# A routed mixture of experts on one core: six single tiles in place of seven, the index table built earlier and in another layout

## The chip, the core and the metric

The kernel runs on one core of a Trainium2 chip. Its engines are TensorE (PE; its weight loads are shown apart as PEld), VectorE (DVE), ScalarE (ACT), GpSimd (POOL) and SyncE (SP). The metric is device time in microseconds (us). A profiled execution gives a trace with the start, the length and the wait of each instruction.

## The reference

`x` has 64 x 64 = 4096 tokens of H = 256 values, and there are E = 8 experts with hidden width M = 512. Each token goes through its two likeliest experts; all is f32.

```python
var = jnp.mean(x * x, axis=-1, keepdims=True)
xn = rms_w * (x * jax.lax.rsqrt(var + EPS))
gate = xn @ wg_W + wg_b + (genre_embed @ gg_W + gg_b)
topk_w, topk_i = jax.lax.top_k(jax.nn.softmax(gate, axis=-1), 2)
cw = jnp.sum(jax.nn.one_hot(topk_i, E) * topk_w[..., None], axis=-2)
h1 = jax.nn.relu(jnp.einsum('bsh,ehm->bsem', x, W1) + b1)
h2 = jax.nn.relu(jnp.einsum('bsem,emn->bsen', h1, W2) + b2)
out_e = jnp.einsum('bsen,enh->bseh', h2, W3) + b3
return x + jnp.einsum('bseh,bse->bsh', out_e, cw)
```

## The kernel before

**Tiles and units.** The 8192 pairs of a token and an expert are sorted by expert and cut into tiles of 128. Token `p * 32 + i` lies in partition `p`, column `i`. The *first part* is columns 0 to 7 (1024 tokens), the rest is columns 8 to 31. The first part is routed first, from its own gates, so that work can begin early: the first `F` units are *single tiles*, unit `u` holding the first 128 pairs of expert `u` from the first part (`firsts` has 128 for experts below `F`, 0 for the others). All other pairs form the *wide units*, after the gates of the rest are known: each expert's remaining tiles are cut into units of four tiles (512 tokens), pairs of tiles, and one last unit of 1 to 4 tiles whose width is a multiple of 32 tokens. `SHAPES` lists the sets of widths for which an arm of the program is written out; which arm runs is read at run time (`nex`). `NREST` is the largest number of tiles that the wide units can have.

**Layers.** A single runs three plain layers (`layer1`: 8 products 128x128, `layer2`: 16 of them, `layer3`: 4 products 128x256). A wide unit runs layers 1 and 2 (`Fast`) with seven products of blocks in place of eight, over half the unit's tokens each (Winograd's form of Strassen's scheme; `fold` makes the sums of weight blocks, `mix` those of data blocks, `p(k)` is a product, `c11`, `c12`, `c22` add them). Layer 3 of a unit of four tiles is of that kind too (`Wide`), of smaller units it is plain. Layer 3 of a unit is done amid the next unit's work.

**The way to the first wide unit.** A generator, `rest()`, issues VectorE's work on the rest in pieces, and `until(label)` in a unit's step runs it up to a label: choice of experts, counts, kinds of units, places. Then the table "slot to token" is built: for each chunk of 16 token columns VectorE makes a one-hot of a pair's row within its tile (`ohl`, from `iotx`), a one-hot of its tile (`ohh`, from `whole`, which `spread_map` makes), and `ohv = ohh * tokw`, with the token numbers `tokw`. TensorE sums 64 products of `ohl` and `ohv` (`table(n)`, the first n columns) in PSUM bank 7. VectorE turns the sum into `idxR`, and GpSimd gathers rows of `x` by it, one indirect DMA per tile: `xgE` for wide unit `F`, the end of `big` for unit `F + 1`, and so on in turn. The rows of unit `F` are transposed on TensorE (eight transposes, four tiles by two halves of H). Those of later units go through DRAM (`stow`, `shuffle`) and VectorE's stream transpose. The weights of the rest's pairs (`pB.weights`, `pB.spread`) are written to `cwdR` in DRAM and gathered by tile (`gather_cw`).

**Order.** Everything is written out by hand (`tc.manual_schedule()`): each engine runs its instructions in the order of the code. `head_step(u)` is the step of singles 0 to `F - 2`, `step(F - 1)` that of the last single, `step_fast(u)` that of a wide unit. SP's queue carries the loads of weights, the copies of `x` into the output (`fill`), the streamed W1 and W3 of the first wide units, and `stow` and `shuffle`; GpSimd's carries gathers and the scatters that add results into the output (`send`). `give` scales a tile's result on VectorE and sends it; `held` keeps some of them for later. A scatter waits for that of the unit before.

Of the kernel before, what the change touches and what calls it, by code (L numbers as in the profile page):

```python
# [52 lines left out]
def kernel(  # L53
# [37 lines left out]
    F = E - 1  # L91
# [556 lines left out]
    def rest():  # L648
# [134 lines left out]
        for c in range(NCH):  # L783
            b0 = HW + (c % 3) * (LW + HW) + LW
            ohv = bigf[:, b0 : b0 + HW].bitcast(F16).rearrange("p (g t) -> p g t", g=GC)
            if c:
# [1 line left out]
            V.tensor_tensor(ohh, whole, hi16[:, cols(c)].unsqueeze(2).to_broadcast([P, GC, NREST]), ALU.is_equal)
# [1 line left out]
            V.tensor_tensor(ohv, ohh, tokw[:, i0 : i0 + GC], ALU.mult)  # L790
# [3 lines left out]
        V.tensor_scalar(sa, tab, 0.0, -1.0, ALU.is_gt, ALU.mult)  # L794
# [15 lines left out]

    def spread_map():
# [981 lines left out]
```

## Time and profile before

| what | value |
|---|---|
| median of 3 runs | 448.67 us (448.43 to 448.75) |
| the profiled execution | 448.61 us |
| its span, first to last instruction | 446.9 us |
| granted TensorE clock | 0.999 |
| busy: PE, PEld, DVE, ACT, POOL | 98%, 91%, 83%, 54%, 63% |
| indirect gathers of x for wide units | 60 |
| indirect gathers of x for singles | 7 |

Rows of a timeline read: start in us, duration in us, engine, line, operation, output <- inputs, shape, number of records merged, and in brackets the idle time before with what ended it. An f32 product is two records. Records overlap on TensorE, so a row's duration is longer than the distance to the next row's start.

### The profile page before, as it was taken

How to read it: one execution, taken by the hardware profiler on the slowest of the kernel's cores; microseconds unless marked ns; L12 is line 12 of the kernel's file. 1: busy time of each engine (PE TensorE's matmuls, PEld its weight loads, DVE VectorE, ACT ScalarE, POOL GpSimd, SP SyncE). 2: the span in 40 equal slices, each digit the busy share in tenths (PEclk: the TensorE clock that was granted, in tenths of full speed). 3: DMA queues.
4: the chain of work that ended last, by engine and by line, in shares of the span. 5: the costliest groups of instructions: out<-in, count | busy, mean ns of one | idle time of the engine just before them, and what ended most of it. 6: DMA issues, size and time to landing. Idle time of an engine off the chain costs nothing. (4 is left out here: it accounts for less than half of the span.)

```text
span 446.9 us, 9223 instructions
## 1 busy us (share of the span) xinstructions
PE 438.7 (98%) x2941; PEld 408.6 (91%) x2941; DVE 369.5 (83%) x967; ACT 242.2 (54%) x572; POOL 279.8 (63%) x237
## 2 busy tenths in 40 slices
PE   9999998999999999999999999999999999999995
PEld 8699997889898999989899999999999889999994
DVE  6898957697979888897979797988877879889962
ACT  5855533547382746555564737474454465655561
POOL 7846316778788877575858483848857447764323
PEclk9999999999999999999999999999999999999999
DMA  8999999579568575455547363736756545766312
GB/s 310 331 352 393 369 364 354 142 229 216 175 126 200 118 162 150 120 120 150 120 126 150 85 150 70 172 92 145 164 149 137 143 117 130 186 169 168 72 15 50
DMA packets 75983, 78.11 MB, mean 175 GB/s; under 512 B 35471, under 2 KB 64114, under 8 KB 75796
## 3 DMA queue, kind: packets, MB, share of 16 engines
q1 hardware_dynamic: 49376, 42.51, 30.0%
q0 software_dynamic: 14912, 17.60, 22.8%
q10 hardware_dynamic: 11636, 17.32, 11.9%
q8 instruction: 25, 0.41, 0.4%
q14 instruction: 34, 0.28, 0.2%
HBM read 61.81 MB, written 20.25 MB: 184 GB/s over the span
## 5 line engine op out<-in xcount | busy, mean ns | idle before, releaser
L1349 POOL DMA_INDIRECT out_dram<-ys,idxR x60 | 97.9, 1632 | 88.6 <-DVE ys L1335 46.8
L1166 PE MATMUL pb<-hid,big 128*128 128x256 f32 (+7 forms) x456 | 84.6, 329 | 0.0
L1187 ACT ACTIVATE hid<-hid,bb 128x256 f32<-128x256 f32 (+12 forms) x152 | 73.1, 530 | 15.5 <-DVE hid L1184 6.3
L874 POOL DMA_INDIRECT cg<-cwdR,idxR x60 | 67.4, 1123 | 19.9 <-issue 17.7
L1166 PEld LDWEIGHTS pb<-hid,big 128*128 128x128 f32 x456 | 72.1, 191 | 4.9 <-issue 0.8
L1175 ACT COPY q1s<-pb 128x512 f32<-128x512 f32 (+7 forms) x57 | 27.5, 482 | 62.1 <-PE pb L1166 61.2
L1166 PE MATMUL pb<-mixB,big 128*128 128x256 f32 (+7 forms) x304 | 56.3, 328 | 0.0
L1175 ACT COPY big<-pb 128x512 f32<-128x512 f32 (+7 forms) x57 | 27.5, 482 | 52.1 <-PE pb L1166 52.1
L1166 PE MATMUL pb<-hotA,big 128*128 128x256 f32 (+7 forms) x304 | 53.2, 328 | 0.0
L1288 PE MATMUL pb<-w3r,hid 128*128 128x256 f32 (+1 forms) x216 | 51.2, 381 | 0.0
L1166 PEld LDWEIGHTS pb<-mixB,big 128*128 128x128 f32 x304 | 48.5, 191 | 2.8
L1166 PEld LDWEIGHTS pb<-hotA,big 128*128 128x128 f32 x304 | 47.9, 191 | 2.9
L1166 PE MATMUL pb<-mixX,iotx 128*128 128x256 f32 (+7 forms) x228 | 46.9, 328 | 0.0
L874 POOL DMA_INDIRECT xgE<-in_x_dram,idxR x32 | 35.8, 1119 | 17.6 <-DVE ib L802 8.2
L1288 PEld LDWEIGHTS pb<-w3r,hid 128*128 128x128 f32 (+1 forms) x216 | 39.1, 190 | 5.2 <-issue 0.8
L1166 PEld LDWEIGHTS pb<-mixX,iotx 128*128 128x128 f32 x228 | 37.4, 191 | 2.5 <-ACT q1s L1175 0.2
L874 POOL DMA_INDIRECT big<-in_x_dram,idxR x28 | 32.2, 1149 | 8.5 <-issue 7.9
L1187 ACT ACTIVATE hid<-pb,bb 128x256 f32<-128x256 f32 (+7 forms) x76 | 27.8, 417 | 15.3 <-PE pb L1166 12.6
L1166 PE MATMUL pb<-xT,w1r 128*128 128x256 f32 (+7 forms) x152 | 31.2, 328 | 0.0
L929 DVE STREAM_TRANSPOSE xT<-gTs 128x256 f32<-128x256 f32 x56 | 29.5, 632 | 0.0
L1067 PE MATMUL pb<-hid,w2a 128*128 128x128 f32 x224 | 27.1, 276 | 0.0
L1067 PEld LDWEIGHTS pb<-hid,w2a 128*128 128x128 f32 x224 | 26.4, 192 | 0.3
(342 smaller groups left out, 841.8 us busy)
## 6 DMA issues: line engine op xcount, KB each, us to landing
w3r<-in_L_cond_W_dram ACTq DMA_DIRECT2D x17, 512.0 KB, 4.7
w2a<-in_L_cond_W_dram SPq DMA_DIRECT2D x8, 1024.0 KB, 13.7
w1r<-in_L_cond_W_dram ACTq DMA_DIRECT2D x16, 512.0 KB
w1r<-in_L_cond_W_dram SPq DMA_DIRECT2D x10, 512.0 KB, 9.5
w3r<-in_L_cond_W_dram SPq DMA_DIRECT2D x9, 512.0 KB, 12.3
big<-in_x_dram SPq DMA_DIRECT2D x8, 512.0 KB, 5.4
gTs<-scr SPq DMA_DIRECT2D x8, 512.0 KB, 4.5
out_dram<-in_x_dram SPq DMA_DIRECT2D x4, 768.0 KB
```

What stands on the lines that cost most here:

```text
L874: return nc.gpsimd.indirect_dma_start(out=dst, out_offset=None, in_=src, in_offset=bass.IndirectOffsetOnAxis(ap=index(b), axis=0), bounds_ ...
L929: V.transpose(xT[:, :, s0 + k, :].rearrange("p c (b k) -> p k c b", b=SQ), shs[:, s0 + k].rearrange("p k (a c) -> p k c a", a=SQ),)
L1067: nc.tensor.matmul(ph, lhsT=w2[:, m, ts(n, P)], rhs=hid[0][:, m, 0:BT], start=(m == 0), stop=(m == MC - 1))
L1166: nc.tensor.matmul(bank[:, ts(n, self.w)], lhsT=w[:, c, ts(n, P)], rhs=x[:, c], start=new and n == 0 and c == 0, stop=n == HB - 1 and c == ...
L1175: nc.scalar.copy(self.q[(1, 6, 5).index(k)], self.tall(self.X if k == 5 else self.U))
L1187: nc.scalar.activation(out, src, AF.Relu, bias=ww[self.u][1][:, self.l, n : n + 1])
L1288: nc.tensor.matmul(sums(u, k)[0 : cols.stop - cols.start], lhsT=hid[1][:, n, cols], rhs=w3[:, n, :], start=(i == 0), stop=(i == MC - 1))
L1349: add = nc.gpsimd.indirect_dma_start(out=orows, out_offset=bass.IndirectOffsetOnAxis(ap=index(b)[0:n], axis=0), in_=y[0:n], in_offset=None ...
```

## The change

`F` goes from 7 to 6. Expert 6 loses its single tile, and its pairs all go to wide units; `SHAPES` is drawn up anew for this (26 rows as before; one shown). In `whole`, `tokw`, `ohh` and `ohv` the axes are exchanged: 16 token columns are now innermost and tiles outside, so a product's moving operand `ohv[:, :, g]` is read with a step of 16 elements of two bytes. Table products and their one-hot rows are placed earlier against the units: chunk 0 ahead of layer 2 of unit 4, chunks 1 and 2 inside it, chunk 3 after layer 1 of unit 5. The weights of the rest and their spread come before the indices, on VectorE with the DMA on SP's queue, not on GpSimd after the gathers. The copy of the first part's weights into `cw8B` moves to the head of the program. In the first wide unit the transposes are done two tiles at a time, with half a layer 3 and products 1 and 2 between.

```diff
-    (5, 6, (16, 15, 15, 14, 12, 11, 10, 9)),
+    (5, 6, (16, 16, 15, 15, 14, 11, 10, 9)),
...
-    F = E - 1
+    F = E - 2
...
-    whole = const.tile([P, GC, NREST], F16, name="whole")
+    whole = const.tile([P, NREST, GC], F16, name="whole")
...
-                [[1, NI], [0, NREST]],
+                [[0, NREST], [1, NI]],
...
-        def spread(self, cwd, cw8, i0):
+        def spread(self, cwd, cw8, i0, eng=nc.gpsimd, queue=nc.gpsimd):
...
-            V.tensor_tensor(ohh, whole, hi16[:, cols(c)].unsqueeze(2).to_broadcast([P, GC, NREST]), ALU.is_equal)
+            V.tensor_tensor(ohh, whole, hi16[:, cols(c)].unsqueeze(1).to_broadcast([P, NREST, GC]), ALU.is_equal)
             i0 = c * GC % NI
-            V.tensor_tensor(ohv, ohh, tokw[:, i0 : i0 + GC], ALU.mult)
+            V.tensor_tensor(ohv, ohh, tokw[:, :, i0 : i0 + GC], ALU.mult)
             for g in range(GC):
-                mms.append((ohls[c][:, :, g], ohv[:, g, :], c * GC + g))
+                mms.append((ohls[c][:, :, g], ohv[:, :, g], c * GC + g))
             yield f"chunk{c}"
+        pB.weights()
+        pB.spread(cwdR, cw8B, 0, V, nc.sync)
+        yield "spread"
...
-        pB.weights()
-        nc.gpsimd.tensor_copy(cw8B[:, 0:NA, :], pA.cw8)
-        pB.spread(cwdR, cw8B, 0)
-        yield "spread"
...
+    def transpose_two(u, k0):
+        tps = [PB[4], PB[7]]
+        for k in (k0, k0 + 1):
+            for c in range(HC):
+                g = xgR[(u - F) % 2][:, k]
                 nc.tensor.transpose(tps[c][:, ts(k, BT)], g.rearrange("p (r c) -> p c r", c=HC)[:, c], ident)
+        for c in range(HC):
+            (nc.scalar.copy if c else V.tensor_copy)(
+                xT[:, c, k0 : k0 + 2, :], tps[c][:, k0 * BT : (k0 + 2) * BT].rearrange("p (s t) -> p s t", s=2)
+            )
...
+    KNOWN = 5
...
-            layer3_of(u - 1, range(HB))
             ranks_of_rest()
-            layer3_of(u - 1, range(HB, MC))
             until("kinds")
...
+        elif u == 4:
+            until("chunk0")
+            table(GC)
+            until("chunk1")
+            until("chunk2")
+            layer2(u, {2: lambda: table(2 * GC), 3: lambda: table(3 * GC)})
...
+    def rows_of_rest():
+        until("chunk3")
+        until("spread")
+        table()
+        until("fetched")
...
             layer1(u)
+            if u == KNOWN:
+                rows_of_rest()
+                stow(F + 1)
+                shuffle(F + 1)
...
         if u == F:
-            transpose_x(u)
+            f = Fast(u, 0)
+            transpose_two(u, 0)
+            scaled(u - 1, "A")
+            layer3_of(u - 1, range(HB))
+            f.p(1)
+            f.p(2)
+            f.c11()
+            transpose_two(u, 2)
+            f.mix(1)
+            f.mix(2)
...
         pA.spread(cwdA, pA.cw8, 0)
+        nc.gpsimd.tensor_copy(cw8B[:, 0:NA, :], pA.cw8)
```

VectorE around the last chunk of one-hot rows. L779 makes `ohl`, L788 `ohh`, L790 `ohv` (all in `big`); `sa` and `idxR` are the indices; L1335 is the update of a tile's result; `denB`, `d2B`, `cw8B` are the weights of the rest. Before:

```order
L779 TENSOR_TENSOR big<-iotx,lo_574 128x2048
L788 TENSOR_TENSOR big<-whole,hi_575 128x1120
L790 TENSOR_TENSOR big<-big,xgE 128x1120
L794 TENSOR_SCALAR sa<-pb_75 128x70
L795 TENSOR_SCALAR sb<-pb_75 128x70
L796 SCALAR_TENSOR_TENSOR sa<-pb_75,sa 128x70
L797 TENSOR_TENSOR idxR<-sa,sb 128x70
```

After:

```order
L1335 SCALAR_TENSOR_TENSOR ys<-pb_73,cg,bc_645 128x256
L1335 SCALAR_TENSOR_TENSOR ys<-pb_74,cg,bc_646 128x256
L779 TENSOR_TENSOR big<-iotx,lo_575 128x2048
L788 TENSOR_TENSOR big<-whole,hi_576 128x1136
L790 TENSOR_TENSOR big<-big,xgE 128x1136
L446 TENSOR_REDUCE denB<-wB 128x24
L447 RECIPROCAL denB<-denB 128x24
L448 TENSOR_TENSOR d2B<-d2B,denB 128x24
L452 TENSOR_TENSOR cw8B<-ohB,denB 128x192
L453 TENSOR_TENSOR wB<-ohB,d2B 128x192
L454 TENSOR_TENSOR cw8B<-cw8B,wB 128x192
L797 TENSOR_SCALAR sa<-pb_75 128x71
```

Two updates (units 2 and 3) and the weights with their spread now stand on VectorE ahead of the indices; before, they came behind them, the spread on GpSimd.

TensorE at the first wide unit. `xgE` holds its gathered rows, `pb_72` and `pb_75` are PSUM banks 4 and 7, L1295 is half a layer 3 of the last single, L1166 a product of the wide unit's layer 1. Before:

```order
L941 MATMUL pb_72<-ident,xgE 128x128 x4
L941 MATMUL pb_75<-ident,xgE 128x128 x4
L1295 MATMUL pb_73<-w3r_86,hid_91 128x256 x2
L1166 MATMUL pb_68<-xT,w1r_83 128x256 x2
L1166 MATMUL pb_69<-mixX,iotx 128x256 x2
L1166 MATMUL pb_70<-xT,w1r_83 128x256 x2
L1166 MATMUL pb_68<-mixX,iotx 128x256 x2
```

After:

```order
L943 MATMUL pb_72<-ident,xgE 128x128
L943 MATMUL pb_75<-ident,xgE 128x128
L943 MATMUL pb_72<-ident,xgE 128x128
L943 MATMUL pb_75<-ident,xgE 128x128
L1295 MATMUL pb_74<-w3r_88,hid_91 128x256 x2
L1166 MATMUL pb_68<-xT,w1r_82 128x256 x2
L1166 MATMUL pb_70<-xT,w1r_82 128x256 x2
L943 MATMUL pb_72<-ident,xgE 128x128
L943 MATMUL pb_75<-ident,xgE 128x128
L943 MATMUL pb_72<-ident,xgE 128x128
L943 MATMUL pb_75<-ident,xgE 128x128
L1295 MATMUL pb_74<-w3r_88,hid_91 128x256 x2
```

Half of a layer 3 and products 1 and 2 now stand between the transposes of tiles 0 and 1 and those of tiles 2 and 3.

GpSimd from the last scatter ahead of the wide units' gathers. `xgE` and `big` take rows of `x` for the first and the second wide unit, `cg` takes weights by tile, `out_dram` is a scatter. Before:

```order
L1349 DMA out_dram<-ys,idxA 4096x256
L874 DMA xgE<-in_x_dram,idxR 128x256 x4
L874 DMA big<-in_x_dram,idxR 128x256 x4
L1349 DMA out_dram<-ys,idxA 4096x256
L807 COPY cw8B<-cw8A 128x64
L452 TENSOR_TENSOR cw8B<-ohB,denB 128x192
L453 TENSOR_TENSOR wB<-ohB,d2B 128x192
L454 TENSOR_TENSOR cw8B<-cw8B,wB 128x192
L455 DMA cwdR<-cw8B 128x256
L874 DMA cg<-cwdR,idxR 128x8 x4
```

After:

```order
L1349 DMA out_dram<-ys,idxA 4096x256 x2
L873 DMA xgE<-in_x_dram,idxR 128x256 x4
L873 DMA big<-in_x_dram,idxR 128x256 x4
L873 DMA cg<-cwdR,idxR 128x8 x4
L1349 DMA out_dram<-ys,idxA 4096x256
L873 DMA xgE<-in_x_dram,idxR 128x256 x4
```

The spread's four rows and its DMA are gone from between the gathers of `x` and those of the weights, and so is a scatter.

More of the change, by code (lines that the diff above doesn't have):

```diff
@@ L770, in rest @@
         LW, HW = P * GC // 2, NREST * GC // 2
-        ohh = bigf[:, 0:HW].bitcast(F16).rearrange("p (g t) -> p g t", g=GC)
+        ohh = bigf[:, 0:HW].bitcast(F16).rearrange("p (t g) -> p t g", g=GC)
         def cols(c):
@@ L814, in spread_map @@
         nc.tensor.matmul(wide, lhsT=place.to_broadcast([P, P]), rhs=ident[:, 0:NREST], start=True, stop=True)
-        nc.scalar.copy(whole, wide.unsqueeze(1).to_broadcast([P, GC, NREST]))
+        nc.scalar.copy(whole, wide.unsqueeze(2).to_broadcast([P, NREST, GC]))
     def ranks_of_rest():
@@ L883 @@
     xgE = buf(run, [P, max(SLOTS * H, NI * NREST // 2)], "xgE")
-    tokw = xgE[:, 0 : NI * NREST // 2].bitcast(F16).rearrange("p (i t) -> p i t", i=NI)
+    tokw = xgE[:, 0 : NI * NREST // 2].bitcast(F16).rearrange("p (t i) -> p t i", i=NI)
     xgR = [
@@ L933, in transpose_x @@
             return
-        if u < F:
-            tps = [PB[4][:, c * BT : (c + 1) * BT] for c in range(HC)]
-        else:
-            tps = [PB[4], PB[7]]
         for c in range(HC):
-            for k, b in enumerate(bs):
-                g = ring(run, [P, H], "xg", 3, b) if u < F else xgR[(u - F) % 2][:, k]
-                nc.tensor.transpose(tps[c][:, ts(k, BT)], g.rearrange("p (r c) -> p c r", c=HC)[:, c], ident)
-            if u == F:
-                (nc.scalar.copy if c else V.tensor_copy)(
-                    xT[:, c, slots(u), :], tps[c].rearrange("p (s t) -> p s t", s=w)
-                )
-        if u < F:
-            nc.scalar.copy(xT[:, :, s0, :], PB[4][:, 0 : HC * BT].rearrange("p (c t) -> p c t", c=HC))
+            g = ring(run, [P, H], "xg", 3, u)
+            nc.tensor.transpose(PB[4][:, ts(c, BT)], g.rearrange("p (r c) -> p c r", c=HC)[:, c], ident)
+        nc.scalar.copy(xT[:, :, s0, :], PB[4][:, 0 : HC * BT].rearrange("p (c t) -> p c t", c=HC))
+    def transpose_two(u, k0):
[3 more added lines that the diff above has]
+                g = xgR[(u - F) % 2][:, k]
+                nc.tensor.transpose(tps[c][:, ts(k, BT)], g.rearrange("p (r c) -> p c r", c=HC)[:, c], ident)
+        for c in range(HC):
+            (nc.scalar.copy if c else V.tensor_copy)(
+                xT[:, c, k0 : k0 + 2, :], tps[c][:, k0 * BT : (k0 + 2) * BT].rearrange("p (s t) -> p s t", s=2)
+            )
     def arena(t, sizes):
@@ L1409, in head_step @@
             scaled(u - 1, "A")
-        if u == F - 2:
-            until("chunk1")
-            table(2 * GC)
         if u == 2:
-            layer3_of(u - 1, range(HB))
             ranks_of_rest()
-            layer3_of(u - 1, range(HB, MC))
             until("kinds")
-        else:
-            layer3(u - 1)
+        if u == KNOWN:
+            rows_of_rest()
+        layer3(u - 1)
         if u - 1 + RING < F:
@@ L1425, in head_step @@
             nc.sync.dma_start(b3_sb[:, u + 2 : u + 4], b3[u + 2 : u + 4].unsqueeze(0).to_broadcast([P, 2, H]))
-        if u == F - 2:
-            until("chunk2")
-            table(3 * GC)
-            until("chunk3")
-            layer2(u, {2: table})
-            until("fetched")
-            stream_3(F, mybir.EngineType.SP)
-            fill(1)
-            stream_1(F + 1, mybir.EngineType.SP)
-            stow(F + 1)
-            shuffle(F + 1)
-            give(u - 2)
-            give(u - 1, held=held)
-            until("spread")
-            return
         if u == 2:
@@ L1449, in head_step @@
             scaled(0, "A")
-        if u != F - 3:
+        if u < F - 3:
             give(u - 1)
@@ L1454, in head_step @@
         if u == F - 3:
-            until("chunk0")
             stream_1(F, mybir.EngineType.SP)
             fill(0)
+        if u == F - 2:
+            stream_3(F, mybir.EngineType.SP)
+            fill(1)
+            stream_1(F + 1, mybir.EngineType.SP)
+            give(u - 2)
+            give(u - 1, held=held)
+            if u == KNOWN:
+                stow(F + 1)
[5 more added lines that the diff above has]
+        until("fetched")
     def fill(k):
@@ L1480, in step @@
             layer1(u)
+            if u == KNOWN:
+                rows_of_rest()
+                stow(F + 1)
+                shuffle(F + 1)
             if u >= F:
@@ L1539, in step_fast @@
         if u == F:
-            scaled(u - 1, "A")
-            layer3_of(u - 1, range(HB))
-            f.p(1)
-            f.mix(1)
+            layer3_of(u - 1, range(HB, MC))
             f.p(5)
-            f.mix(2)
-            f.mix(3)
-            f.p(2)
-            f.c11()
             f.mix(4)
             f.p(6)
+            f.mix(3)
             f.p(3)
@@ L1556, in step_fast @@
             f.r22()
-            layer3_of(u - 1, range(HB, MC))
             f.p(4)
```

10 lines of the change are left out of this document (5 added, 5 removed), and 50 rows, old and new, of the table SHAPES.

## The prediction

> **What bounds the kernel now.** I read the page first, then TensorE in order of time, then what ends its only long wait (the queue of GpSimd's gathers, VectorE ahead of them, the DMA load), then the shapes of the wide units.
>
> ```profile
> span 446.9 us, 9223 instructions
> PE 438.7 (98%) x2941; PEld 408.6 (91%) x2941; DVE 369.5 (83%) x967; ACT 242.2 (54%) x572; POOL 279.8 (63%) x237
> ```
>
> TensorE is busy for 98% of the span, and its timeline names no idle time between 79 us and its last product. So the time is TensorE's work, plus its waits before 79 us, plus an end that the change leaves alone. The profiled execution took 448.61 us, its span and 1.7 around it; the median of the runs is 448.67, 0.06 more, and I count from the median. About 0.2%, 0.9 us, is what a measurement tells from no change.
>
> Rows are start, duration, engine, line and operation. A product in f32 is two records, and I take the cost of a piece as the distance between starts. First one single tile (unit 4), undisturbed:
>
> ```profile
> 49.74 1.95 PE L1057 MATMUL pb<-xT,w1r 128*128 128x128 f32 x16
> 51.53 0.40 PE L941 MATMUL pb<-ident,xg 128*128 128x128 f32 x2
> 51.76 1.89 PE L1288 MATMUL pb<-w3r,hid 128*128 128x256 f32 x8
> 53.49 3.73 PE L1067 MATMUL pb<-hid,w2a 128*128 128x128 f32 x32
> 57.06 1.95 PE L1057 MATMUL pb<-xT,w1r 128*128 128x128 f32 x16
> ```
>
> A single costs 57.06 - 49.74 = 7.32 us: layer 1 1.79, two transposes 0.23, a layer 3 1.73, layer 2 3.57. The wait is at the first wide unit, unit 7:
>
> ```profile
> 75.60 0.28 PE L941 MATMUL pb<-ident,xgE 128*128 128x128 f32 x1
> 76.36 0.39 PE L941 MATMUL pb<-ident,xgE 128*128 128x128 f32 x1 [0.48 <-DMA xgE<-in_x_dram,idxR]
> 78.25 0.86 PE L941 MATMUL pb<-ident,xgE 128*128 128x128 f32 x5 [0.88 <-DMA xgE<-in_x_dram,idxR]
> 78.95 1.03 PE L1295 MATMUL pb<-w3r,hid 128*128 128x256 f32 x4
> ```
>
> From 75.60 to 78.95 eight transposes pass, 0.92 us of work by the 0.23 for two. The other 2.43 us are spent on rows of x still in flight. This is the wait that the change moves.
>
> **The change, part by part.**
>
> *The seventh single goes: -7.32 us.* Its 128 pairs go to the wide units. Routing the reference's input by its gate, I find that expert 6 has 639 pairs left over before and 767 after: a pair of tiles and a last unit of three tiles (width 12, 384 tokens), then a pair and a last unit of four (width 16, 512 tokens). The other experts keep their units, 19 in all. The widths 16, 15, 15, 14, 12, ... that this gives for before are those of the trace's shapes (half a width is one product's columns).
>
> *That unit widens.* The rows are layer 2 at 256 and at 192 columns, then two consecutive products of the four-tile layer 3:
>
> ```profile
> 88.71 3.62 PE L1166 MATMUL pb<-hotA,big 128*128 128x256 f32 x16
> 301.99 2.76 PE L1166 MATMUL pb<-hotA,big 128*128 128x192 f32 x16
> 103.39 1.05 PE L1256 MATMUL pb<-w3r,hid 128*128 128x128 f32 x8
> 104.28 1.06 PE L1256 MATMUL pb<-graw,hotA 128*128 128x128 f32 x8
> ```
>
> (3.62 - 2.76) / 8 = 0.1075 us more for each of 14 + 28 products: +4.52. Layer 3 was three tiles at 1.73, 5.19 in all; it becomes seven products at 104.28 - 103.39 = 0.89, 6.23: +1.04. So TensorE's work falls by 7.32 - 4.52 - 1.04 = 1.76 us. The tiles to gather, scale and scatter stay at 67, so GpSimd's count there is unchanged.
>
> *What the wait becomes.* The chain is: one-hot rows on VectorE, table products on TensorE, indices on VectorE, gathers on GpSimd, landing.
>
> ```profile
> 49.34 1.22 DVE L779 TENSOR_TENSOR big<-iotx,lo 128x2048 f16<-128x2048 f16 x1
> 50.47 1.32 DVE L788 TENSOR_TENSOR big<-whole,hi 128x1120 f16<-128x1120 f16 x1
> 51.83 0.74 DVE L790 TENSOR_TENSOR big<-big,xgE 128x1120 f16<-128x1120 f16 x1
> 52.48 1.22 DVE L779 TENSOR_TENSOR big<-iotx,lo 128x2048 f16<-128x2048 f16 x1
> 66.57 1.13 PE L646 MATMUL pb<-big 128*128 128x70 f16 x16
> 67.53 1.14 PE L1067 MATMUL pb<-hid,w2a 128*128 128x128 f32 x8
> 67.74 0.23 DVE L794 TENSOR_SCALAR sa<-pb 128x70 f32<-128x70 f32 x1 [4.25 <-PE pb L646]
> 31.87 0.62 DVE L404 TENSOR_TENSOR ohB<-gTs 128x192 f32<-128x192 f32 x1
> 69.00 0.87 DVE L1335 SCALAR_TENSOR_TENSOR ys<-pb,cg,bc 128x256 f32<-128x256 f32 x2
> 70.60 0.35 DVE L1031 TENSOR_SCALAR bc<-b_sb,cg 128x256 f32<-128x256 f32 x1
> ```
>
> A chunk takes VectorE 3.14 us (49.34 to 52.48). The comparison with `whole` takes 1.32 for 1120 elements with the repeated operand innermost; the one with `iotx`, whose repeat is in the middle, 1.22 for 2048. In the new layout both are of the second kind, so I price the first at 0.75, like the product's 0.74: a chunk takes 2.57. The counts also come half a layer 3 (0.87) sooner, and unit 2's update (0.4, half of the 0.87 that two take) no longer stands ahead of chunk 0. From 48.1, four chunks, two updates before the last and a short wait for `whole` make chunk 3 ready at about 59.4. Weights and spread now stand on VectorE ahead of the indices: 0.7 for the weights (69.00 to 70.60 without the two updates) and three rows over 192 elements, at most 0.62 each by a row of that size (L404). They end at about 62.0.
>
> TensorE from 49.74: layer 1, transposes, layer 3, chunk 0's products (16 take 67.53 - 66.57 = 0.96), layer 2 with chunks 1 and 2 inside, layer 1 of unit 5, chunk 3. With 0.25 for the splits that is 13.2 us, to 62.94. So TensorE and not VectorE ends this stretch, and the weights hide. If that cover is gone (VectorE at its old 3.14 a chunk), the indices come 1.4 later.
>
> ```profile
> 52.36 1.11 POOL L874 DMA_INDIRECT xg<-in_x_dram,idxA  x1 [0.31 <-issue]
> 58.85 0.40 PE L941 MATMUL pb<-ident,xg 128*128 128x128 f32 x2
> 59.00 1.61 POOL L1349 DMA_INDIRECT out_dram<-ys,idxA  x1 [5.53 <-DVE big L790]
> 68.78 1.04 POOL L874 DMA_INDIRECT xgE<-in_x_dram,idxR  x1 [8.18 <-DVE ib L802]
> 70.13 1.01 POOL L874 DMA_INDIRECT xgE<-in_x_dram,idxR  x1 [0.30 <-issue]
> 72.75 1.15 POOL L874 DMA_INDIRECT xgE<-in_x_dram,idxR  x1 [0.30 <-issue]
> 79.05 0.99 POOL L874 DMA_INDIRECT big<-in_x_dram,idxR  x1 [0.30 <-issue]
> 81.99 0.38 SPq L913 DMA_DIRECT2D scr<-big  x1
> ```
>
> Before, the first gather starts 1.25 after the table products' slot ends (67.53 to 68.78). After: 62.94 + 1.25 = 64.19, and the second tile's gather 1.35 later, at 65.54. GpSimd is free by then: unit 2's scatter (59.00) ends at 60.6. TensorE is ready for the first two tiles after a layer 3 and a layer 2, at 62.94 + 1.73 + 3.57 = 68.24.
>
> Landing, from a gather's start to the use that waited for it: second tile 76.36 - 70.13 = 6.2, fourth 78.25 - 72.75 = 5.5. The DMA engines are full there (share is the column before GB/s):
>
> ```profile
> 72.00:74.00 2.00, 2.00 (x19) 1.97 (x19) 2.00 (x5) 0.37 (x1) 1.60 (x2) 1.00 1.02 404
> 74.00:76.00 2.00, 1.87 (x17) 1.68 (x16) 1.93 (x5) 0.88 (x3) 1.52 (x1) 1.00 0.91 366
> 76.00:78.00 2.00, 0.77 (x2) 0.39 (x2) 1.18 (x2) 0.23 (x1) 1.66 (x2) 1.00 0.46 166
> ```
>
> The backlog ends near 75.7. The change drops one W1 and one W3, 1 MB at the 366 to 404 GB/s of these rows, so it ends some 2.7 us sooner, near 73.0; the new gathers lie wholly within it. With 5.8 us the second tile lands at 71.35. TensorE has waited 3.1 less the first tile's transposes, 2.87. Turning by twos means that tiles 2 and 3 (landed by 73.7) get half a layer 3 and two products as cover, 2.6 us, and are not waited for. But product 5 then waits behind VectorE's sum, copy and subtraction, about 0.45. Wait after: 3.3; before: 2.43; +0.9.
>
> *Other edits.* The copy of the first part's weights on GpSimd moves to the head, into a stretch where GpSimd waits for the write of those weights: nothing, and its own length if a gather of x behind it were waited for. The spread's DMA moves to the sync queue, behind the last loads. It must land before the weights' gathers, which GpSimd reaches only after eight gathers of x, near 75; the backlog ends before that. If not, GpSimd waits with nothing urgent behind it.
>
> *Sum.* -1.76 + 0.89 = -0.87: 447.8 us. The single's 7.3 us shrink because 5.6 return in the wide unit, and half of the rest goes into a longer wait for the same gathers, which are issued 4.6 us sooner to a TensorE that is ready 7.4 sooner.
>
> *Strided moving rows.* The products' moving operand, contiguous before, is now read at 32 bytes a column. The stationary one is so already:
>
> ```profile
> L646 PEld LDWEIGHTS <-big 128*128 128x128 f16 x64 | 4.4, 165 | 0.1
> L419 PEld LDWEIGHTS <-tri 128*128 128x128 f16 x2 | 0.2, 98 | 0.0
> ```
>
> A load and a product together take 0.96 / 16 = 60 ns, so the spaced load costs little in pace although its row is 67 ns longer than the contiguous one. I take nothing. Upper end: those 67 ns for 128 columns, 37 for 71, uncovered on 64 products, +2.4. Less than nothing is excluded, since as many columns are read.
>
> The Trainium skill ("SBUF — State Buffer", Door 1: The DMA port swizzle) speaks against this edit: SBUF has 16-byte lines, and every access that crosses to a new line pays. By it the 64 products would pay on each column; the pace of the spaced loads here does not show a large penalty.
>
> **The rivals.**
>
> *Early rows.* If the gathers land as they do without load (79.05 to 81.99, 2.94), the second tile is there at 68.5 and VectorE is late next:
>
> ```profile
> 76.49 0.68 DVE L1124 TENSOR_TENSOR big<-big 128x512 f32<-128x512 f32 x1
> ```
>
> Its folds end 9.4 us after L794; 1.6 of that (69.00 to 70.60) has moved ahead. From 63.1 they end at 70.9, and then the copy lets product 1 start at 71.4, a wait of 1.85 + 0.45. Time 446.8. Against it: full DMA engines at 64 to 71 us.
>
> *Late rows (slower).* If gathers land only when the backlog runs out (the second landed 0.6 after 75.7), the second tile comes at 73.6, 2.25 later than I say: 450.05. It decides above a landing time of 7.6 us (+1.8 over mine). For it: the tiles landed in a row as the load fell. Against: the gather at 52.36 was used at 58.85 without a wait, so it landed within 6.5 us, under full load and behind a scatter.
>
> The Trainium skill ("DMA: Bandwidth & Descriptors", Queues, rings and completion order) says that each engine goes round its queues packet by packet. By it a gather is not held until another queue is empty; the 6.5 agrees.
>
> *Slow table products (slower).* The 2.4 us above, and the gathers later with them: 450.2, and on this side of no change from 14 ns a product.
>
> *No gain by design.* If the wider unit cost more than the single, the sum would turn; this needs 0.15 us instead of 0.1075 a product, and no row says so.
>
> **How the numbers follow.** Forecast 0.60: landing 5.4 to 6.3 and copies 0.3 either way give 447.2 to 448.4; not quite half of it lies beyond 0.9 us. Early rows 0.15. Late rows 0.12, a third of it within 0.9. Slow products 0.10, three tenths of it within. Anything else 0.03. Faster: 0.29 + 0.15 = 0.44. Same: 0.31 + 0.04 + 0.03 + 0.01 = 0.39. Slower: 0.17. The range takes in early rows with half a microsecond below, and both slower rivals: 446.2 to 450.2.
>
> **What would show it.** One 192-column unit fewer and one 256-column unit more; comparisons with `whole` near 0.75 us; sixteen table products still 0.96 apart; first gather near 64.2; transposes of the first wide unit starting near 68.2, held until about 71.4 by DMA, the second two tiles without a DMA wait; layer 2 of that unit near 80.5. I am wrong if the landing is not 5.4 to 6.3 us, if VectorE rather than TensorE ends ahead of the indices, or if a new wait appears after 80 us.

## The result: 1.1% slower, and the profile after

The changed kernel takes 453.45 us (median of 4 runs, 452.79 to 453.95) against 448.55 (448.03 to 448.75) for the kernel before, run beside it: a ratio of 1.011 [1.0093, 1.0128]. I had said 447.8, with 450.2 as the upper end. The profiled execution took 453.71 us, 5.10 more than the profiled one of before. The kernel before took 464.5 us beside e1 to e4 and 462.4 beside e16 and e17, against 448.1 to 448.5 beside the other experiments, so these six are read by their ratios and by single durations alone. From the page of the changed kernel:

```profile
span 452.0 us, 9182 instructions
PE 442.2 (98%) x2915; PEld 410.5 (91%) x2915; DVE 374.1 (83%) x982; ACT 242.7 (54%) x570; POOL 279.7 (62%) x233
```

TensorE is busy 3.5 us longer, though it has 26 records fewer. TensorE's timeline from unit 4 to layer 2 of the first wide unit shows where (the last row is the last layer 3 of all):

```profile
50.39 1.95 PE L1057 MATMUL pb<-xT,w1r 128*128 128x128 f32 x16
54.14 2.35 PE L646 MATMUL pb<-big 128*128 128x71 f16 x16
56.31 2.86 PE L1067 MATMUL pb<-hid,w2a 128*128 128x128 f32 x24
66.03 2.33 PE L646 MATMUL pb<-big 128*128 128x71 f16 x16
68.19 1.91 PE L1288 MATMUL pb<-w3r,hid 128*128 128x256 f32 x8
75.02 0.47 PE L943 MATMUL pb<-ident,xgE 128*128 128x128 f32 x2 [1.36 <-DMA xgE<-in_x_dram,idxR]
75.80 0.50 PE L943 MATMUL pb<-ident,xgE 128*128 128x128 f32 x2 [0.30 <-DMA xgE<-in_x_dram,idxR]
80.54 1.99 PE L1166 MATMUL pb<-mixX,iotx 128*128 128x256 f32 x8 [0.31 <-DVE mixX L1149]
85.12 1.13 PE L1166 MATMUL pb<-mixX,w1r 128*128 128x256 f32 x4 [0.78 <-DVE hid L1184]
86.09 1.89 PE L1166 MATMUL pb<-hid,big 128*128 128x256 f32 x8
443.18 3.62 PE L1288 MATMUL pb<-w3r,hid 128*128 128x256 f32 x16
```

The rows of before for the end of this stretch, and its last layer 3:

```profile
84.13 1.11 PE L1166 MATMUL pb<-mixX,iotx 128*128 128x256 f32 x4
85.07 1.03 PE L1295 MATMUL pb<-w3r,hid 128*128 128x256 f32 x4
86.99 1.89 PE L1166 MATMUL pb<-hid,big 128*128 128x256 f32 x8
438.36 3.62 PE L1288 MATMUL pb<-w3r,hid 128*128 128x256 f32 x16
```

Sixteen table products take 56.31 - 54.14 = 2.17 us, where they took 0.96: 136 ns each instead of 60. Four such slots cost 4.8 us more. The waits that these rows name are 1.36 + 0.30 + 0.31 + 0.78 = 2.75 us, where those of before name 0.48 + 0.23 + 0.88 = 1.59 (the prediction's 2.43 also has the gaps too short to be named). Layer 2 of the first wide unit starts at 86.09, only 0.90 sooner than before, and from there to the end of the span it is 365.9 us against 359.9, 6.0 more: 5.72 up to the last layer 3 (357.09 against 351.37), and 0.28 behind its start.

VectorE and GpSimd show what the slow products hold up:

```profile
62.01 0.36 DVE L454 TENSOR_TENSOR cw8B<-cw8B,wB 128x192 f32<-128x192 f32 x1
68.40 0.23 DVE L797 TENSOR_SCALAR sa<-pb 128x71 f32<-128x71 f32 x1 [6.04 <-PE pb L646]
69.45 1.08 POOL L873 DMA_INDIRECT xgE<-in_x_dram,idxR  x1 [9.36 <-DVE ib L805]
```

VectorE is done with the spread at 62.4, as forecast (62.0), and then stands still for 6.04 us until the slow products end. The gathers start at 69.45, not 64.19. TensorE is late by as much: it is ready for the rows at 69.93 + 3.57 = 73.50, not 68.24. So the rows are not waited for longer.

### The profile page after: what moved, and what is told of

It reads as the page before. It is cut to its first block, busy times and chain, and to the rows that moved or that the text cites. A ratio compares the mean times of both kernels' runs of the same rounds, so it can differ in the third digit from the quotient of the medians.

```text
span 452.0 us, 9182 instructions
## 1 busy us (share of the span) xinstructions
PE 442.2 (98%) x2915; PEld 410.5 (91%) x2915; DVE 374.1 (83%) x982; ACT 242.7 (54%) x570; POOL 279.7 (62%) x233
## 5 line engine op out<-in xcount | busy, mean ns | idle before, releaser
L1166 PE MATMUL pb<-hid,big 128*128 128x256 f32 (+6 forms) x456 | 85.9, 331 | 0.0
L1187 ACT ACTIVATE hid<-hid,bb 128x256 f32<-128x256 f32 (+11 forms) x152 | 73.8, 534 | 15.6 <-DVE hid L1184 4.9
L1166 PEld LDWEIGHTS pb<-hid,big 128*128 128x128 f32 x456 | 72.6, 191 | 5.4 <-issue 0.8
L1175 ACT COPY q1s<-pb 128x512 f32<-128x512 f32 (+6 forms) x57 | 27.8, 487 | 63.5 <-PE pb L1166 62.8
L1166 PE MATMUL pb<-mixB,big 128*128 128x256 f32 (+6 forms) x304 | 57.1, 331 | 0.0
L1175 ACT COPY big<-pb 128x512 f32<-128x512 f32 (+6 forms) x57 | 27.8, 487 | 51.3 <-PE pb L1166 50.5
L1166 PE MATMUL pb<-hotA,big 128*128 128x256 f32 (+6 forms) x304 | 54.0, 331 | 0.0
L1166 PEld LDWEIGHTS pb<-mixB,big 128*128 128x128 f32 x304 | 48.8, 191 | 3.2
L1166 PEld LDWEIGHTS pb<-hotA,big 128*128 128x128 f32 x304 | 48.3, 191 | 3.3
L1166 PE MATMUL pb<-mixX,iotx 128*128 128x256 f32 (+6 forms) x228 | 47.4, 331 | 0.3 <-DVE mixX L1149 0.3
L1166 PEld LDWEIGHTS pb<-mixX,iotx 128*128 128x128 f32 x228 | 37.4, 191 | 3.3 <-DVE mixX L1149 0.7
L1187 ACT ACTIVATE hid<-pb,bb 128x256 f32<-128x256 f32 (+6 forms) x76 | 27.9, 418 | 16.6 <-PE pb L1166 13.5
L1166 PE MATMUL pb<-xT,w1r 128*128 128x256 f32 (+6 forms) x152 | 31.5, 331 | 0.0
L1166 PEld LDWEIGHTS pb<-xT,w1r 128*128 128x128 f32 x152 | 25.3, 191 | 1.8
L1033 ACT ACTIVATE bc<-b_sb,cw 128x256 f32 x59 | 25.5, 500 | 1.0 <-issue 0.4
```

The lines of the kernel that those rows point to most:

```text
L1033: nc.scalar.mul(bc, b3e, cw)
L1166: nc.tensor.matmul(bank[:, ts(n, self.w)], lhsT=w[:, c, ts(n, P)], rhs=x[:, c], start=new and n == 0 and c == 0, stop=n == HB - 1 and c == ...
L1175: nc.scalar.copy(self.q[(1, 6, 5).index(k)], self.tall(self.X if k == 5 else self.U))
L1187: nc.scalar.activation(out, src, AF.Relu, bias=ww[self.u][1][:, self.l, n : n + 1])
```

## Experiments

**What the step of the moving operand costs.** e1 undoes the layout alone:

```diff
-    whole = const.tile([P, NREST, GC], F16, name="whole")
+    whole = const.tile([P, GC, NREST], F16, name="whole")
...
-                mms.append((ohls[c][:, :, g], ohv[:, :, g], c * GC + g))
+                mms.append((ohls[c][:, :, g], ohv[:, g, :], c * GC + g))
```

> The changed kernel with the one-hot layout of before (moving operand contiguous, VectorE's comparison at its old form), all else as changed. Theory: the loss is TensorE's time on 64 products whose moving operand is read 32 bytes a column (a slot of 16 takes 2.17 us instead of 0.96, 4.8 us in all). Then the slots are back at 0.96, VectorE's comparison at 1.32, VectorE ends ahead of the indices at about 64.6 us, and the time is 448.0 to 449.3 us. Rival: the loss comes from the new order (fewer singles, products earlier, rows later). Then the slots fall back too but the time stays above 451.5 us.

470.43 us, ratio to before 1.0131 [1.0074, 1.0188]. The slots are 0.96 again. The comparison on VectorE is 1.33 again, so chunk 3 comes 0.97 us late, and TensorE waits 2.84 us for rows. The layout is not the whole loss, as the rival has it.

e2 groups the token columns by twos (a step of 4 bytes), e3 puts the new layout into the kernel before, e4 groups by fours (8 bytes):

```diff
-            ohv = bigf[:, b0 : b0 + HW].bitcast(F16).rearrange("p (t g) -> p t g", g=GC)
+            ohv = bigf[:, b0 : b0 + HW].bitcast(F16).rearrange("p (b t g) -> p b t g", b=GC // ST, g=ST)
...
-                [[0, NREST], [1, NI]],
+                [[ST, NI // ST], [0, NREST], [1, ST]],
...
-                mms.append((ohls[c][:, :, g], ohv[:, :, g], c * GC + g))
+                mms.append((ohls[c][:, :, g], ohv[:, g // ST, :, g % ST], c * GC + g))
```

> The changed kernel with two token columns innermost instead of sixteen: VectorE's rows keep a run of two, the moving operand is read at 4 bytes a column. If only wide steps cost TensorE time: slots of 16 products at 0.96 us, comparisons at 0.75, time 447.5 to 448.7 us (my forecast, plus up to 0.6 for the later arrival of x at the start that the changed kernel's profile shows). If any step off contiguous costs 75 ns a product: slots at 2.17 and 453.4 us.

482.88 us, ratio 1.0407 [1.0348, 1.0465], a miss, and not by the products, whose slots are 0.97. GpSimd's timelines (e2, then the changed kernel) show the reason:

```profile
10.75 25.45 POOL L307 IOTA xgE<- 64x2272 f16 x2
36.38 1.12 POOL L878 DMA_INDIRECT xg<-in_x_dram,idxA  x1 [0.18 <-issue]
```
```profile
11.70 4.79 POOL L306 IOTA xgE<- 64x2272 f16 x2
```

The token numbers written in runs of two take GpSimd 25.45 us for the same elements, and the next gather of the head waits behind them.

> The kernel before with the new one-hot layout alone (16 token columns innermost). Stride theory: slots of 16 products at 2.17 us, indices some 4.8 us later, time 451.3 to 453.4 us (the wait for the first wide rows may shrink by up to 2 us, since the loads are over when the gathers start). Rival, that the loss is the order's: 448 to 449 us.

470.93 us, ratio 1.011 [1.0065, 1.0154]. No durations are taken from this run; e8 below repeats it. The layout costs the kernel before about as much as the whole change costs.

> As the run at 4 bytes, with four columns innermost: 8 bytes a column. If the price starts where fewer than two columns share 16 bytes: slots still 0.96 us and the time as at 4 bytes. If the price grows with the step: slots between 0.96 and 2.17 us, near 1.25 if in proportion, and about 1.2 us more time than at 4 bytes.

466.37 us, one run. TensorE's rows:

```profile
61.17 1.31 PE L647 MATMUL pb<-big 128*128 128x71 f16 x16
62.30 2.90 PE L1072 MATMUL pb<-hid,w2a 128*128 128x128 f32 x24
```

A slot is 62.30 - 61.17 = 1.13, 71 ns a product, with VectorE's comparison at 0.74.

e5 keeps the token numbers as in the changed kernel and regroups them in the multiply (step 4 bytes); e6 repeats e1, e7 puts e5's layout and e8 the 32 bytes into the kernel before, all on one chip:

```diff
-            V.tensor_tensor(ohv, ohh, tokw[:, :, i0 : i0 + GC], ALU.mult)
+            V.tensor_tensor(ohv, ohh, tokw[:, :, i0 : i0 + GC].rearrange("p t (b g) -> p b t g", g=ST), ALU.mult)
```

> The changed kernel with two token columns innermost (moving operand read at 4 bytes a column), the token numbers kept as in the changed kernel so that GpSimd's writing of them stays at 2.4 us a half (the first run at 4 bytes had made it 12.7). Theory (the loss is the wide step): slots of 16 products 0.96 to 0.97 us, comparisons 0.75, indices about 63.7 us, time 447.3 to 449.0 us. Rival (the order loses time by itself): slots the same, time above 451 us.

> The changed kernel with the layout of before, once more, since the granted clock had fallen in the first run of it (0.98). Theory: 448.0 to 449.5 us, some 0.5 us over the run at 4 bytes, as VectorE's comparisons at 1.33 us end 1 us after TensorE needs the last chunk. Rival (the order loses by itself): above 451 us.

> The kernel before (seven singles, its own order) with two token columns innermost. Its last chunk waits for TensorE's place in the order, not for VectorE, so the faster comparisons should gain nothing: 448.2 to 448.9 us, the same as before. If VectorE's chunks did bound the indices: 446.5 to 447.5.

> The kernel before with the change's layout alone, once more for the same reason. Stride theory: slots of 16 products 2.17 us, time 451.3 to 453.4 us. Rival, that the loss is the order's: 448 to 449 us.

| run | step, order | us | ratio to before | one slot |
|---|---|---|---|---|
| e5 | 4 bytes, new | 451.92 | 1.0075 [1.005, 1.0101] | 0.97 |
| e6 | contiguous, new | 452.32 | 1.009 [1.0064, 1.0117] | 0.96 |
| e7 | 4 bytes, before | 449.11 | 1.0022 [1.0006, 1.0038] | 0.97 |
| e8 | 32 bytes, before | 453.73 | 1.0123 [1.009, 1.0156] | 2.15 |

So the step of 32 bytes alone costs the old order 1.2%, and the new order without it still loses 0.75 to 0.9%. e7 and e8 lie 0.2 and 0.3 us above the ranges in their texts. Grouping by twos is not free on VectorE in this form: the multiply that regroups takes 1.14 us in e5 instead of 0.75, so a chunk takes 2.97, against 2.58 in the changed kernel and 3.17 in e6. The 0.17 a chunk that this saves in e7 (3.14 before) is worth nothing in the old order.

e15 takes 16 bytes, in a single run (452.09 us):

> The changed kernel with the moving operand at 16 bytes a column; one look, for the pace of the table products alone. So far 60 ns a product at 2 and 4 bytes, 71 at 8, 135 at 32. Theory 1 (the price rises with the step): 85 to 105 ns, 1.4 to 1.7 us for 16. Rival (it is paid in full as soon as each column lies in a 16-byte line of its own, as the Trainium skill's page SBUF — State Buffer, Door 1, has it): 135 ns, 2.16 us for 16. The whole 451 to 453.5.

```profile
53.27 2.31 PE L647 MATMUL pb<-big 128*128 128x71 f16 x16
55.40 2.86 PE L1072 MATMUL pb<-hid,w2a 128*128 128x128 f32 x24
```

A slot is 2.13, 133 ns a product. By step, then: 2 bytes 60, 4 bytes 61, 8 bytes 71, 16 bytes 133, 32 bytes 136. The price does not rise evenly with the step; it jumps between 8 and 16. That is the rule of the Trainium skill ("SBUF — State Buffer", Door 1: The DMA port swizzle), which asks for at least two hits on each 16-byte line; the small price at two hits (11 ns) is not in it, and where it puts the stride that is free at 8 elements of bf16, the 133 ns at 8 elements of f16 speak against it.

**Why the new order loses without that price.** e5's TensorE timeline:

```profile
64.73 3.73 PE L1072 MATMUL pb<-hid,w2a 128*128 128x128 f32 x32
70.74 0.67 PE L948 MATMUL pb<-ident,xgE 128*128 128x128 f32 x2 [2.28 <-DMA xgE<-in_x_dram,idxR]
72.47 0.70 PE L948 MATMUL pb<-ident,xgE 128*128 128x128 f32 x2 [1.06 <-DMA xgE<-in_x_dram,idxR]
72.97 1.91 PE L1300 MATMUL pb<-w3r,hid 128*128 128x256 f32 x4
74.67 3.20 PE L1171 MATMUL pb<-xT,w1r 128*128 128x256 f32 x8
77.71 0.63 PE L948 MATMUL pb<-ident,xgE 128*128 128x128 f32 x4
85.07 1.89 PE L1171 MATMUL pb<-hid,big 128*128 128x256 f32 x8
```

TensorE stands still for 3.34 us, and then works at half pace: half a layer 3 takes 74.67 - 72.97 = 1.70 instead of 0.87, two products 3.04 instead of 1.73. In the rows by stage the granted clock, the number after the five engines, says so:

```profile
68.00:70.00 2.00, 0.46 (x5) 0.27 (x3) 0.93 (x2) 0.40 (x2) 1.48 (x2) 1.00 1.08 420
70.00:72.00 2.00, 0.67 (x2) 0.31 (x2) 1.93 (x5) 0.00 (x0) 1.70 (x2) 0.62 1.03 411
72.00:74.00 2.00, 1.53 (x5) 1.35 (x6) 1.48 (x3) 0.78 (x2) 1.69 (x2) 0.50 0.96 367
74.00:76.00 2.00, 2.00 (x7) 1.53 (x6) 0.00 (x0) 0.00 (x0) 1.04 (x2) 0.50 0.48 160
76.00:78.00 2.00, 2.00 (x9) 1.67 (x8) 0.02 (x1) 0.58 (x1) 1.00 (x1) 0.67 0.27 78
```

The slowed pieces lose 0.83 + 1.31 = 2.14 us. The Trainium skill ("TensorE: Matmul & The Clock Gate", Part 1: The HAM clock gate) has a rule of this kind: TensorE falls to half its clock after an idle window of about 3.4 us. I had not drawn on it. The trace differs in the time: a mean of 0.62 from 70.00 to 72.00 means full clock until about 70.5, and TensorE had stood still only since 70.74 - 2.28 = 68.46. So the clock fell after about 2 us of standing still, within the first of the two waits. e9 fills the wait with products whose result nobody reads, e12 with the single's whole layer 3:

```diff
+            for _ in range(8):
+                keep_busy()   # ident x ident, into an unread part of PSUM bank 6
             transpose_two(u, 0)   # four more keep_busy() inside, between its tiles
```
```diff
+            layer3_of(u - 1, range(MC))
             transpose_two(u, 0)
             scaled(u - 1, "A")
-            layer3_of(u - 1, range(HB))
...
-            layer3_of(u - 1, range(HB, MC))
```

> Base: the changed kernel with the moving operand at 4 bytes (451.92 us; TensorE waits 2.28 and 1.06 us for rows of x, then half a layer 3 takes 1.70 instead of 0.865 and products 1 and 2 take 3.04 instead of 1.73 at a granted clock of 0.5). Edit: twelve products of the identity with itself, 0.22 us each, into a bank part that nobody reads: eight before the first two transposes of the first wide unit, four between the tiles. They take no rows and no operand away. Theory 1 (the clock is halved because TensorE stood still): half a layer 3 near 0.87, products 1 and 2 near 1.73, granted clock 1.0 throughout, and 449.3 to 450.3 in all. Rival (the slow stretch comes from something else that happens then, as full DMA engines): the 1.70 and 3.04 stay, and the time is 451.5 to 452.5.

450.16 us, ratio 1.0031 [1.0017, 1.0044]. From its timeline:

```profile
72.43 1.03 PE L1305 MATMUL pb<-w3r,hid 128*128 128x256 f32 x4
74.58 1.99 PE L1176 MATMUL pb<-xT,w1r 128*128 128x256 f32 x8 [1.13 <-DVE xT L955]
76.41 0.63 PE L953 MATMUL pb<-ident,xgE 128*128 128x128 f32 x4
83.77 1.89 PE L1176 MATMUL pb<-hid,big 128*128 128x256 f32 x8
```

The two products take 1.83, the clock stays at 1.00 in every stretch, with the DMA engines as full as in e5, and no run has a mean clock below 0.997, where e5's lie at 0.991 to 0.995. Standing still costs the clock. Part of the gain is given back at once: VectorE's copy of the first tiles stands behind the sums for layer 2, and TensorE now waits 1.13 for it.

> Same base. Edit: all four columns of the last single tile's layer 3 (1.73 us) stand ahead of the first transposes, none behind. Theory 1 (standing still halves the clock): TensorE then stands still for at most 0.6 and 1.1 us, no half clock (2.15 less), 1.73 us of waiting filled, but no cover for the copies: 0.4 before product 1 and 0.9 before product 5. 449.2 to 450.2. Rival (the clock falls for another reason): 451.3 to 452.3 with products 1 and 2 again near 3 us.

452.53 us, ratio 1.0076 [1.0052, 1.01]. The text of theory 1 was wrong by size:

```profile
71.71 0.50 PE L948 MATMUL pb<-ident,xgE 128*128 128x128 f32 x2 [0.81 <-DMA xgE<-in_x_dram,idxR]
74.50 3.78 PE L1171 MATMUL pb<-xT,w1r 128*128 128x256 f32 x8 [2.29 <-DVE xT L950]
```

With its layer 3 gone, TensorE waits 2.29 for that same copy, not 0.4, and the clock is halved again (this execution, at 455.09 us, is the longest of the six). Most of this standing still was for VectorE, so it is not only waits for DMA that cost the clock.

e14 puts e9's products into the wait of the kernel before, two ahead of each tile:

> The kernel before, with eight products of the identity with itself (0.22 us each) between the transposes of its first wide unit, two ahead of each tile, where it waits 2.43 us for rows. Of 28 runs of the kernel before on this chip and another, 19 had a granted clock of 0.998 or more and a median of 448.26 us, 9 one of 0.994 to 0.996 and 450.31. Theory 1 (standing still for that long sometimes halves the clock for some 4 us): the runs at 0.996 and below vanish, and all lie at 448.0 to 448.8. Rival (these runs are slower for a reason that lies elsewhere): a quarter to a third of the runs still are at 450.

448.66 us, ratio 1.0004 [0.999, 1.0018]; all 12 runs have a mean clock of 0.997 or more and lie at 448.24 to 449.29, where 3 of the 17 of before beside them are at 0.994 to 0.996 and 449.72 to 450.75. That fits the theory, but 3 of 17 is little to have vanished, and the median gains nothing.

**What holds the rows.** e10 moves the first two fills behind the load of the next W1, e11 also gives both copies of the first two tiles to ScalarE. The wait that e10's text speaks of fell on an earlier gather, which had landed; what ran is fills issued at 61 us instead of 55 and 59.

```diff
-            fill(1)
             stream_1(F + 1, mybir.EngineType.SP)
+            fill(0, fetches[-5])
+            fill(1)
...
-            (nc.scalar.copy if c else V.tensor_copy)(
+            (nc.scalar.copy if c or k0 == 0 else V.tensor_copy)(
```

> Same base. Edit: the first two of the four late copies of x into the output (fills, 0.79 MB each, issued on the sync queue at 55 and 59 us) are issued behind the load of the next W1 and wait until the fourth gather of the first wide unit has landed. Theory 1 (rows land late because of the loads ahead of them): 1.6 MB at about 400 GB/s are 3.9 us less in front of the gathers, they land 3 to 4.5 us after their issue instead of 6 to 7, and the first transposes start before 69.5 instead of at 70.74. VectorE is then late next, since its copy of the first tiles stands behind the sums for layer 2 (ending 73.1): product 1 cannot start before 71.5 to 73.5, and the whole is 449.5 to 451.5. Rival (each gather has a latency of 6 to 7 us whatever else moves): transposes again at 70.7 and 72.5, 451.9 within 0.7.

> As the run with the later fills, and both copies of the first two turned tiles go to ScalarE, which stands idle there, instead of one to VectorE behind the sums. If the rows come early and VectorE was late next, product 1 starts by 71, no wait of TensorE reaches 2 us, the clock stays, and the time is 446.8 to 449 (451.9 less 3.3 of waiting, less 2.15 of half clock, plus some 1 to 1.5 of shorter waits that stay). If VectorE was not the next to be late, the same as the run with the later fills within 0.5.

450.46 us, ratio 1.0036 [1.0017, 1.0055], and 449.94, 1.0024 [1.0006, 1.0042]. The waits for rows are 2.6 and 2.75 us, and both scatter with the clock: e11's six runs at 0.997 or more take 448.94 to 449.43, the six at 0.993 to 0.995 take 450.44 to 451.11. The loads being ahead, VectorE's sums end sooner (70.9 instead of 73.1), and the copies' move makes no difference beyond the error. Theory 1 was missed in both: the first transposes of e10 start at 70.45, not before 69.5, and e11 does not reach 446.8 to 449.

e13 is e11 with the fills waiting for the fourth gather (the two calls stand behind `rows_of_rest()` in unit 5's step):

> Base: the changed kernel with the moving operand at 4 bytes and both copies of the first two turned tiles on ScalarE. In the earlier run with later fills the two fills had only moved behind the load of the next W1, to 61 us, still ahead of the gathers; here their issue waits until the fourth gather of the first wide unit has landed. Theory 1 (the rows are late because of the loads issued ahead of them): 1.6 MB at about 400 GB/s are 3.9 us less ahead of the gathers; the first transposes start by 69.2 instead of 70.25, the second by 70.5, TensorE waits under 1.5 us there instead of 2.7, the clock stays in most runs, layer 2 of that unit starts at 79 to 81, and the time is 447.0 to 448.8. Rival (the gathers take their 5 to 6 us whatever is in flight): transposes at 70.2 and 71.5, 449 to 450.

452.0 us, ratio 1.0075 [1.0053, 1.0097]. Its rows are a gather, the transposes and the fills:

```profile
64.39 1.08 POOL L878 DMA_INDIRECT xgE<-in_x_dram,idxR  x1 [3.63 <-DVE ib L810]
70.31 0.48 PE L948 MATMUL pb<-ident,xgE 128*128 128x128 f32 x2 [1.65 <-DMA xgE<-in_x_dram,idxR]
72.31 1.17 SPq L1466 DMA_DIRECT2D out_dram<-in_x_dram  x2
```

The fills are out of the way until 72.31, and still 5.9 us pass from the gather to its use (6.0 in e11, 6.6 in e5). The rival's times hold: this time does not shrink when 1.6 MB leave the queues. That it would not shrink whatever is in flight is not shown, since other transfers still keep the DMA engines full until 69 (share 1.04 from 68 to 69). The total misses both texts. Of the 4.2 us by which this execution is longer than e11's, 1.45 lie before layer 2 of the first wide unit, where the clock is halved again, and the rest behind it. There the fills stand ahead of the next unit's rows on SP's queue, whose store goes out at 81.26 instead of 77.68; that this is the cause was not tested.

**Asking sooner.** e16 takes e11 and asks for the rows sooner, with new cover for the two later waits; e17 adds five products in the wait; e18 is e16 once more on another chip.

```diff
-            layer1(u)
-            if u == KNOWN:
-                rows_of_rest()
+            layer1(u, rows_of_rest if u == KNOWN else None)   # after half of layer 1
...
             f.p(1)
-            f.p(2)
-            f.c11()
             transpose_two(u, 2)
+            f.p(2)
...
             f.r22()
+            layer3_of(u - 1, range(HB, MC))
             f.p(4)
```

Besides, `pB.weights` and `pB.spread` stand behind the indices.

> Base: the changed kernel with the moving operand at 4 bytes, the first two fills behind the load of the next W1 and both copies of the first two turned tiles on ScalarE (449.94 us; its runs at a granted clock of 0.997 or more 448.9 to 449.5, the others 450.4 to 451.1). Edits: the last 16 table products stand after half of unit 5's layer 1 instead of behind all of it, and weights and spread go behind the indices on VectorE, so that the gathers start 1 us sooner (63.1 to 63.3 instead of 64.24); product 2 stands behind the second two transposes as their cover, and the second half of layer 3 between products 7 and 4, where TensorE waited 0.78 for VectorE. Theory 1 (the rows' landing after a fixed 5.7 to 6.5 us, the clock that falls on waiting, and the lost cover are all that the new order loses): first transposes near 69.3, second near 70.5, wait for rows 1.4 to 2.0 instead of 2.7, no wait of 0.78, the clock at 0.997 or more in most runs, layer 2 of that unit at 79.8 to 81, 447.0 to 448.3. Rival (the rows wait for the DMA engines to come free, near 70 to 72, whenever they are asked for): first transposes again at 70.2, half the clock in half of the runs, 448.5 to 450.

> As the run with sooner gathers and cover, with five products of the identity with itself: two before the first transposes, three between the tiles. If its clock holds anyway, the same within 0.3; if half of its runs lose it, this one is 0.5 to 1.5 lower and has no run at a clock of 0.995.

> The same kernel as in the run with sooner gathers and cover, since there the chip ran every kernel slowly (the kernel before 462.4 instead of 448.3 us) and the profiled execution was a disturbed one, so that the times of its first wide unit tell nothing. Expected as before: gathers from 63.2, first transposes near 69.3 and second near 70.5 by theory 1, 447.0 to 448.3 in all; 70.2 and 448.5 to 450 by the rival.

e16: ratio 0.9953 [0.9915, 0.9991]; e17: 0.9958 [0.9926, 0.999], both beside runs of the kernel before from 460.57 to 465.67 us, which is too wide to tell what e17's products do. e18: 448.38 us (447.99 to 449.3), ratio 0.9998 [0.9985, 1.0011]. Its GpSimd and TensorE:

```profile
63.52 1.08 POOL L877 DMA_INDIRECT xgE<-in_x_dram,idxR  x1 [4.30 <-DVE ib L807]
69.62 0.47 PE L947 MATMUL pb<-ident,xgE 128*128 128x128 f32 x2 [0.91 <-DMA xgE<-in_x_dram,idxR]
70.90 0.51 PE L947 MATMUL pb<-ident,xgE 128*128 128x128 f32 x2 [0.81 <-DMA xgE<-in_x_dram,idxR]
73.84 0.50 PE L947 MATMUL pb<-ident,xgE 128*128 128x128 f32 x2 [0.48 <-DMA xgE<-in_x_dram,idxR]
79.86 1.13 PE L1172 MATMUL pb<-mixX,w1r 128*128 128x256 f32 x4
80.83 1.89 PE L1172 MATMUL pb<-hid,big 128*128 128x256 f32 x8
```

The gather goes out 0.72 us sooner than in e11 (64.24) and its tile is used 0.63 sooner (70.25), 6.1 after its issue: the time to landing is the same, so asking sooner pays. The waits are 2.20 us, none is named after 74, and layer 2 starts 6.16 us sooner than before. The rest of the span is 6.0 longer (446.7 - 80.83 = 365.9 against 359.9). So the order can be had without loss, 1.1% better than the changed kernel, but in e18 it does not beat the kernel before, and e16's 0.5% is not confirmed. The transposes are 0.3 and 0.4 later than theory 1 had them, and the time lies just above its range; four of the twelve runs still have a mean clock of 0.995 or 0.996. How much each of the edits gave was not separated.

## Why the prediction was wrong, point by point

- **Table products, "I take nothing": the step that failed.** It measured +4.8 us, twice the "upper end" of 2.4. I argued from weight loads with the same step, which cost little in pace. They could not tell: a load row is 165 ns long where load and product together take 60, so the load runs beside other products, while the moving operand's step set the pace itself (136 ns). The upper end was worked out from the same loads, so it was no bound. The Trainium skill's line rule, which I quoted as speaking against the edit, was right, and I let a row of another kind outweigh it. It was the rival "slow table products", chance 0.10, and its cost of 76 ns a product is far above the 14 at which that rival had the sign turn. But the sign would have been wrong without it too: e5, at 61 ns, is still 0.75% slower.
- **The wait of 3.3 us.** With the price taken away (e5), the steps to it hold: first gather 64.17 (forecast 64.19), TensorE ready at 68.3 (68.24), comparisons by VectorE as priced (0.74 for 0.75). The rows alone are then waited for 3.34 us, where I had 2.87; that 3.34 is close to my 3.3, which had 0.45 before product 5 in it, is luck. And what such a wait does was left out: half the clock, 2.14 us in e5. In the changed kernel itself the slow products came with a wait for rows of only 1.66 us and the clock held, so the two losses partly replace each other: 1.1% with the price, 0.75% without.
- **Landing, 5.8 us.** 5.6 and 5.0 in the changed kernel, 6.6 and 6.9 in e5, 6.1 and 6.0 in e18. The range I gave, 5.4 to 6.3, was too narrow by about half a microsecond on both sides. That the backlog of loads matters was shown wrong for the 1.6 MB of fills (e13); the loads of weights that remained were not taken away.
- **Cover.** The wait before product 5 was 0.31 (forecast 0.45). The 0.78 before product 4 I missed: half a layer 3 stood there before (85.07) and covered VectorE's sum. The diff shows it moving away. I costed where it went, not what it left.
- **TensorE's work, -1.76.** This held. The wider unit and the rest take 5.72 more up to the last layer 3: the 5.56 that I priced, and 0.16 of a new wait for a copy on ScalarE (at 320.63). The single's 7.32 fits the sum below within 0.23. The end, which I took as unchanged, is 0.28 longer. So 1.76 us of work were gained, and in e5 waits and the halved clock, 3.34 + 0.31 + 0.79 + 2.14 = 6.6 against 1.59 of named waits, took them back and more.
- **The sum.** From the end of the last single's layer 2 to layer 2 of the wide unit stand eight transposes (0.92) and nine pieces of 0.865, 8.71 us of work. Before, this stretch takes 86.99 - 75.60 = 11.39, so 2.68 are gaps, named or not; in the changed kernel it takes 86.09 - 73.50 = 12.59, 3.88 of gaps, 1.20 more (forecast 0.89). From layer 1 of unit 4 to layer 2 of the wide unit the changed kernel takes 35.70 us against 37.25, 1.55 less: -7.32 + 4.80 + 1.20 is -1.32, and 0.23 lies in shorter gaps between the pieces. With 0.65 by which this execution was late already at unit 4 (49.66 to 50.41 in e5, e6 and e8; GpSimd starts the token numbers at 11.70 instead of 11.10 already, far ahead of the products), and 6.0 behind, that is the 5.1.

## What to carry to other kernels

Price a strided operand from rows in which that same operand is strided: a moving operand with one element in each 16-byte line more than doubled a 71-column product (60 to 133 ns), while groups of two elements gave VectorE the same faster comparison (0.74 us) at no price on TensorE; check who pays for the regrouping (VectorE's multiply in e5, GpSimd's token numbers in e2). A wait of 2 to 3 us on TensorE can cost more than itself, for half the clock can follow; asking for the rows sooner shortened it (e18), and products in the wait kept the clock (e9). Moving real work into it paid nothing in e12, since that work had covered a copy. When work is moved, name what it covered at its old place.

## What the runs showed of the hardware

- The moving operand's price is a jump, not a slope: 60, 61, 71, 133 and 136 ns a product of 71 columns in f16 at 2, 4, 8, 16 and 32 bytes a column.
- TensorE's clock halved about 2 us into a wait of 2.28 us in e5, and in e13 with waits of 1.65 + 0.72 and two transposes between; with 1.36 + 0.30 it held in the changed kernel, and with 1.72 + 0.86 in e10's profiled execution. So the length of the wait alone does not decide, and the same kernel shows both (e11). What else decides is not shown. The kernel before, which waits 2.43, shows both too: beside e9 to e12, 19 of its 28 runs have a mean clock of 0.998 or more and a median of 448.26 us, 9 have 0.994 to 0.996 and 450.31.
- GpSimd's iota slows as the runs get shorter: 2 x 2272 numbers on 64 partitions take 4.79 us in runs of 32, 9.90 in runs of 4 and 25.45 in runs of 2.
